# Summing the moved tiles of the last attention in SBUF rather than in DRAM

## The chip, the cores and the metric

The kernel runs on one core of a Trainium2 chip. The time is that of the device in microseconds, the median of three runs. TensorE (PE) multiplies matrices, VectorE (DVE) and ScalarE (ACT) work element by element, GpSimd (POOL) here hardly does more than issue transfers, and SyncE (SP) issues the plain loads and stores. Each engine takes its instructions in a fixed order.

## What is computed

Two graph layers on 4096 nodes with 512 features and a dense 4096 x 4096 adjacency mask. The first is an encoder and decoder with sigmoid attention in four heads. The second, in which the change lies, is a graph attention in four heads:

```python
feats  = einsum('nf,hfo->hno', X, W)
e_s    = einsum('hno,ho->hn', feats, a_self)
e_n    = einsum('hno,ho->hn', feats, a_neigh)
logits = e_s[:, :, None] + e_n[:, None, :]
logits = where(logits > 0, logits, 0.2 * logits)
logits = logits + NEG_INF * (1.0 - A)[None]
attn   = softmax(logits, axis=-1)
out    = einsum('hnm,hmo->hno', attn, feats)
out    = relu(out + b)          # then x = x + out
```

For each target node the weights over all source nodes are needed twice: multiplied with the features of the sources, and summed, since the softmax divides by their sum (the denominator).

## The kernel before

Three attentions (encoder, decoder, last) go through one function, `attention`. In the last, called at L788, a block is one head with one half of the targets: 4 heads x 2 halves of `TB` = 2048 targets make eight blocks, n = 0 to 7. A block runs over 32 tiles j of 128 sources. For each tile:

- SP loads a mask tile `a` (L198, 128 x 2048 bytes, five buffers).
- ScalarE makes the weights `e` (L761) from a row of the targets, `rowb`, and a column of the sources. In block 0 `rowb` is `row0`, a view of the tile `w` of 128 x 2048 floats; the later blocks load their own.
- VectorE multiplies by the mask (L762). Below, this is called the weighting of a tile.
- TensorE multiplies the features with the four slices of `e` into PSUM (L332, L329). The profile counts two instructions per product of float32.

The tiles `e` come from a rotation of nine buffers (`weight_tile`, L225).

The denominator is summed in three ways, divided by the constant `GAT` (L64). Tiles 14, 30 and 31 go through TensorE, multiplied by ones (L286). Eleven "moved" tiles (1, 3, 6, 8, 11, 13, 16, 18, 21, 23, 26) are summed by transfers that GpSimd issues (L344): the first is a plain store to `dacc[tb]`, a tile of 1 MiB in DRAM, the other ten add to it. There are two such tiles, one for each half of the targets, and so used by turns. At j = 30 the sum is read back into a weight tile `back` (L302). The other 18 are summed by VectorE into the tile `acc`, here a part of `R` (L350 for the first two, then L352). At the end of a block TensorE multiplies `back` and `acc` by ones as well (L286).

When a block is over, its sums leave PSUM on a chain of small transfers, all on GpSimd's queue, while the next block runs: ScalarE copies the sums (L235), `dens` is stored (L236) and loaded as a column `dcol` (L238), VectorE inverts it (L242, L243), `rinvs` is stored (L244), and four rows `rb` are loaded from it, spread over the partitions, two buffers by turns (L249). VectorE multiplies the block's output by them (L770), ScalarE adds the bias (L773), and GpSimd adds the result to the output in DRAM (L779). The last block ends without this chain.

Where these instructions stand in the order of each engine is decided by a scheduler when the program is built. A few places are tied by hand: `issue_after` keeps products and denominator products in a given order on TensorE.

The constants that matter are

```python
NJ = 32; TB = 2048; EP = 2; EVICT = 2      # e: EP + ebufs = 2 + 7 buffers
GAT = (1, 3, 6, 8, 11, 13, 16, 18, 21, 23, 26), (14, 30, 31)
```

Of the kernel before, what the change touches and what calls it, by code (L numbers as in the profile page):

```python
# [34 lines left out]
ALU = mybir.AluOpType  # L35
# [4 lines left out]
N, F, H, D, P = 4096, 512, 4, 128, 128  # L40
IB = 512
NIB = N // IB
NJ = N // P
C = IB // P

TB = 2048
# [10 lines left out]
TINY = 1e-30  # L57
# [6 lines left out]
GAT = (1, 3, 6, 8, 11, 13, 16, 18, 21, 23, 26), (14, 30, 31)  # L64
# [15 lines left out]
def kernel(ctx, tc, x, xT, adjT, w0, w0T, v0, wencT, wdecT, vecs, w1, w1T, a1, outT):  # L80
    nc = tc.nc
# [7 lines left out]
    R = [big.tile([P, N], FP, name=f"R{i}") for i in range(5)]  # L89
# [59 lines left out]
    dacc = [dram.tile([P, TB], FP, name=f"dacc{n}") for n in range(2)]  # L149
# [49 lines left out]


    def attention(what, keep, pools, weights, values, row_of, out, finish, ebufs, modes=None, invert=None,
                  kept=None, sums=None, extras={}, row0=None, masks0=()):

# [15 lines left out]
        spool, made, masks0 = pools, 0, list(masks0)  # L221
# [54 lines left out]
        for n, (h, tb) in enumerate(blocks):  # L276
            last = n == len(blocks) - 1
            moved, by_ones = modes(n) if modes is not None else ((), ())
            if invert is not None:
                den = bank1()  # L280
                begun = False

            def add_to_den(t, stop=False):
                nonlocal begun, last_ones
                for s in range(SB):
                    last_ones = nc.tensor.matmul(den[s * 32:(s + 1) * 32, :], ones[:, 0:32], t[:, s * IB:(s + 1) * IB],  # L286
                                                 start=not begun, stop=stop)
                begun = True

            po, ahead = [bank() for _ in range(SB - 1)], []  # L290
            adds, held, back, stores, next_row = [], [], None, [], None
            for j in range(NJ):
                for f in later.pop(j, []):
                    f()
                with tc.issue_after(a_load.ins) if j else nullcontext():
                    if (n, j) in extras:
                        extras[n, j]()
                    if not last and j == NJ - 10:
                        next_row = next_row_of(*blocks[n + 1])
                if moved and j == NJ - 2:  # L300
                    back = weight_tile()
                    nc.gpsimd.dma_start(back, dacc[tb])  # L302
                e = weight_tile()
                store = j % KEEP == KEEP - 1 and kept is not None
                if store and kept == "read":
                    a_load = nc.sync.dma_start(e, ekeep[h][tb][j // KEEP])
                else:
                    if masks0:
                        a, a_load = masks0.pop(0)
                    else:  # L310
                        a = mask_tile(keep)
                        a_load = load_mask(a, tb, j)
                    weights(e, rowb, a, j, h, SB if n + j == 0 else 1)
                    if store:
                        stores.append((j // KEEP, e))

                    if j % KEEP == KEEP - 3 and stores:
                        k, t = stores.pop()
                        nc.scalar.dma_start(ekeep[h][tb][k], t)

                def products():
                    nonlocal last_main, last_ones

                    with tc.issue_after(last_ones.ins) if last_ones is not None else nullcontext():

                        if j == EVICT:
                            po.append(bank())
                            for k, t in ahead:
                                nc.tensor.matmul(po[-1], block(values[h], k), t[:, (SB - 1) * IB:SB * IB],  # L329
                                                 start=(k == 0), stop=False)  # L330
                        for s, b in enumerate(po):
                            last_main = nc.tensor.matmul(b, block(values[h], j), e[:, s * IB:(s + 1) * IB],  # L332
                                                         start=(j == 0), stop=(j == NJ - 1))
                    last_ones = None


                early = last and j == NJ - 1 and invert is not None
                if not early:
                    products()
                if j < EVICT:  # L340
                    ahead.append((j, e))
                if invert is not None:
                    if j in moved:
                        nc.gpsimd.dma_start(dacc[tb], e, **({"accum_op": ALU.add} if j > moved[0] else {}))  # L344
                    elif j in by_ones:
                        held.append(e)
                    else:
                        adds.append(e)
                        if len(adds) == 2:
                            nc.vector.tensor_add(acc, *adds)  # L350
                        elif len(adds) > 2:
                            nc.vector.tensor_add(acc, acc, e)  # L352

                    if held and j + 1 not in by_ones:
                        with tc.issue_after(last_main.ins):
                            for t in held:
                                add_to_den(t)
                        held = []
                    if j == NJ - 1:
                        with tc.issue_after(last_ones.ins) if last_ones is not None else nullcontext():  # L360
                            if back is not None:
                                add_to_den(back)
                            add_to_den(acc, True)
                if early:
                    products()
            for k, t in stores:
                if last:
                    nc.scalar.dma_start(ekeep[h][tb][k], t)
                else:
                    at(EVICT, nc.scalar.dma_start, ekeep[h][tb][k], t)  # L370
            if not last:
                at(EVICT, lambda *block_end: ending(*block_end), h, tb, po, den if invert is not None else None)
                rowb = next_row
                continue
            outs = [out(spool, h, tb, s, po[s]) for s in range(SB)]
            if invert is None:
                for s, o in enumerate(outs):
                    rb = spread(h, tb, s)
                    for f in finish:
                        f(spool, h, tb, s, o, rb, True)  # L380
                continue

            inv = spool.tile([P, IB], FP, name="dsb")
            nc.vector.tensor_scalar(inv, den, invert[0], None, invert[1])
            nc.vector.reciprocal(inv, inv)
            if kept is not None:
                nc.gpsimd.dma_start(rinvs[h][tb].rearrange("o (s i) -> (o s) i", i=IB), inv[0:P:32, :])
            for s, o in enumerate(outs):
                rb = bank()
                nc.tensor.matmul(rb, ident[:, 32 * s:32 * s + 1].to_broadcast([P, P]), inv, start=True, stop=True)  # L390
                for f in finish:
                    f(spool, h, tb, s, o, rb, True)
# [13 lines left out]
    with tc.tile_pool(name="keep", bufs=1) as keep:  # L406

        with tc.tile_pool(name="f_small", bufs=1) as small, tc.tile_pool(name="f_work", bufs=2) as work:
# [5 lines left out]
            for ib in range(NIB):  # L414
# [7 lines left out]
                for c in range(0, C, 1 if ib == 0 else C):  # L422
                    n = 1 if ib == 0 else C
# [8 lines left out]
            for ib in range(NIB):  # L432
# [29 lines left out]
                for c in range(C):  # L462
                    j = ib * C + c
# [7 lines left out]
                if ib == SB - 1:  # L471
                    store_rows(rows[0], targets(0))
                    row0 = keep.tile([P, TB], FP, name="rowb", bufs=2)
                    row0_load = load_row(row0, rows[0], 0)
                    with tc.issue_after(row0_load.ins):
                        masks0 = []
# [39 lines left out]
        with tc.tile_pool(name="enc", bufs=1) as spool:  # L516

            with tc.issue_after(last_act.ins), tc.issue_after(masks0[-1][1].ins):
                attention("enc", keep, spool, tanh_weights, R[0:4], lambda h, tb: (rows[tb], h), out_enc,
                          (scaled, statistics), 7, lambda n: ENC if n > 1 else ENC_FIRST, (TINY, ALU.max), "write",  # L520
                          row0=row0, masks0=masks0,
                          extras={(2, 8): encoder_weights, (H * NTB - 1, NJ // 2): three_heads})
# [85 lines left out]
        with tc.tile_pool(name="dec", bufs=1) as spool:  # L608
            attention("dec", keep, spool, tanh_weights, xc, lambda h, tb: (rows[tb], h), out_dec, (scaled, elu), 4,
                      kept="read")  # L610
# [3 lines left out]
    with tc.tile_pool(name="l_small", bufs=1) as small, tc.tile_pool(name="l_work", bufs=2) as work:  # L614
# [82 lines left out]
        for ib in range(NIB):  # L697
            for c in range(C):
# [3 lines left out]
                j = ib * C + c  # L702
# [18 lines left out]
            if ib == SB - 1:  # L721
                store_rows(rows1[0], targets(0))
                row0 = w.rearrange("p c f -> p (c f)")
# [57 lines left out]
    with tc.tile_pool(name="gat", bufs=1) as spool:  # L781
        x1_last = []

        def load_last():
            x1_last.append(spool.tile([P, TB], FP, name="rowb", bufs=2))
            nc.sync.dma_start(x1_last[0], outT[(H - 1) * P:H * P, (NTB - 1) * TB:NTB * TB])

        attention("gat", spool, spool, gat_weights, v1, lambda h, tb: (rowsg, tb * H + h), out_gat,  # L788
                  (scaled_gat, add_to_output), 7, lambda n: GAT, (N * TINY, ALU.add), sums=R[2][:, 0:TB], row0=row0,
                  extras={(H * NTB - 1, NJ - 10): load_last})  # L790


# [40 lines left out]
```

## Time and profile before

| | us |
|---|---|
| median of three runs | 3400.32 |
| lowest, highest | 3393.2, 3400.7 |
| the profiled run, its span | 3400.29, 3398.4 |
| last attention, first weights to the end of the span | 2423.6 to 3398.4 |
| additions and stores to dacc (L344), whole kernel | 142, of 1 MiB each, 8.6 from issue to landing |
| read-backs (L302), whole kernel | 14, of 1 MiB each, 5.3 from issue to landing |

The decoder's attention sums nothing, as it uses what the encoder's kept. So the transfers of L344 and L302 are those of the encoder's and the last attention.

In a line of the timeline the columns are the start, the duration (both in us), the engine, the line of the kernel, the instruction, what it writes and reads and how often; in brackets stands how long the engine was idle before and what ended it. In a line of waits: who waited on which line, for what, how long in all, how often, and the longest. In a line by windows: the stretch, its length, the busy time with the number of instructions, the granted clock of TensorE, the share of the DMA engines and GB/s. The name of what ended a wait is inferred; where the engine named had long been done it was another.

### The profile page before, as it was taken

Reading aid. Unit: us, or ns where it says so; the run is one execution under the profiler, and the core shown is the slowest. Engines: PE = TensorE matmul, PEld = TensorE weight load, DVE = VectorE, ACT = ScalarE, POOL = GpSimd, SP = SyncE. Lnnn points to the kernel's source line nnn. Section 1 sums busy time; section 2 is a strip of 40 time slices with the busy share of each in tenths; the row PEclk is TensorE's granted clock in tenths of the full one; section 3 lists DMA queues with packets and bytes.
Section 4 is the critical chain, followed back from the end, with each engine's and each line's share of the span. In section 5 each row is a group of like instructions: output and inputs, shape, how many; then the busy total and the mean of one; then the engine's idle time right before and its main releaser. Section 6 shows DMA issues by size and latency. Waiting matters only on the chain.

```text
span 3398.4 us, 26074 instructions
## 1 busy us (share of the span) xinstructions
PE 3255.4 (96%) x8943; PEld 1501.3 (44%) x8943; DVE 2679.7 (79%) x1912; ACT 2598.4 (76%) x1908; POOL 325.5 (10%) x479
## 2 busy tenths in 40 slices
PE   7969999999999999999999999989999999999999
PEld 6423344344344464444444444448544344444443
DVE  6969799899898775665666556585699999999998
ACT  7969799999999438999999999565665564656553
POOL 2000000010010000000000000024201111111110
PEclk9989999999999999999999999989999999999999
DMA  9994578778777103434444344231388788788876
GB/s 190 195 158 146 163 225 241 205 214 240 208 227 200 55 13 136 142 130 138 145 141 136 133 139 139 62 127 69 94 206 205 186 216 192 196 207 201 208 187 169
DMA packets 180309, 559.60 MB, mean 165 GB/s; under 512 B 20372, under 2 KB 23700, under 8 KB 144208
## 3 DMA queue, kind: packets, MB, share of 16 engines
q0 software_dynamic: 43232, 211.14, 31.7%
q1 hardware_dynamic: 126288, 293.66, 25.8%
q10 hardware_dynamic: 10656, 53.15, 3.9%
q8 instruction: 70, 1.15, 0.1%
q14 instruction: 63, 0.52, 0.0%
HBM read 391.78 MB, written 233.19 MB: 184 GB/s over the span
## 4 chain that ended last, share of the span: by engine, by line
PE 57%; DVE 19%; DMA 11%; issue 9%; ACT 3%; POOL 1%; DVEq 0%; ACTq 0%; POOLq 0%
PE ps L332 42%; DVE e L762 7%; PE ps L533 6%; DMA a<-mask 5%; DVE R L352 5%; DVE e L402 4%; PE ps L707 3%; DMA rb<-rinvs 3%; DMA rinvs<-dcol 1%; PE den L286 1%; DVE acc L352 1%; ACT e L401 1%; ACT e L400 1%; PE ps L467 1%; PE ps L588 1%
## 5 line engine op out<-in xcount | busy, mean ns | idle before, releaser
L332 PE MATMUL ps<-e,R 128*128 128x512 f32 x6048 | 2661.4, 601 | 104.3 <-DVE e L402 70.9
L332 PEld LDWEIGHTS ps<-e,R 128*128 128x128 f32 x6048 | 1155.8, 192 | 1600.2 <-issue 1437.4
L402 DVE TENSOR_TENSOR e<-e,a 128x2048 f32<-128x2048 f32 (+1 forms) x470 | 1050.2, 2259 | 372.5 <-ACT e L401 348.3
L400 ACT ACTIVATE e<-rowb,score 128x2048 f32<-128x2048 f32 (+1 forms) x470 | 913.5, 1968 | 82.4 <-PE ps L332 46.6
L401 ACT ACTIVATE e<-e 128x2048 f32<-128x2048 f32 (+1 forms) x470 | 872.8, 1882 | 44.1 <-DVE e L402 37.6
L761 ACT ACTIVATE e<-rowb,nq,jcol 128x2048 f32<-128x2048 f32 x224 | 454.6, 2085 | 206.9 <-DMA dacc<-e 165.0
L762 DVE SCALAR_TENSOR_TENSOR e<-e,jcol,a 128x2048 f32<-128x2048 f32 (+1 forms) x259 | 589.7, 2316 | 3.8 <-DMA a<-mask 2.6
L352 DVE TENSOR_TENSOR R<-R,e 128x2048 f32<-128x2048 f32 x128 | 291.5, 2278 | 0.0
L352 DVE TENSOR_TENSOR acc<-acc,e 128x2048 f32<-128x2048 f32 x126 | 288.1, 2287 | 2.2
L344 POOL DMA_DIRECT2D dacc<-e x142 | 117.8, 830 | 1087.9 <-DMA dacc<-e 432.7
L533 PE MATMUL ps<-R,w 128*128 128x512 f32 x512 | 220.3, 592 | 0.6 <-DVE w L501 0.6
L249 POOL DMA_DIRECT2D rb<-rinvs x88 | 47.9, 547 | 1135.4 <-DVE R L491 874.5
L533 PEld LDWEIGHTS ps<-R,w 128*128 128x128 f32 x512 | 97.2, 190 | 122.7 <-issue 117.9
L773 ACT ACTIVATE R<-R,vec 128x512 f32<-128x512 f32 x32 | 23.1, 722 | 142.2 <-DVE R L770 141.7
L707 PE MATMUL ps<-w1x,hT 128*128 128x260 f32 x512 | 117.5, 388 | 2.8 <-ACT hT L683 2.8
L553 ACT ACTIVATE ex<-ps,bias 128x512 f32<-128x512 f32 x64 | 44.1, 688 | 97.5 <-PE ps L533 80.4
L707 PEld LDWEIGHTS ps<-w1x,hT 128*128 128x128 f32 x512 | 97.7, 193 | 22.8 <-ACT hT L683 4.4
L286 PE MATMUL den<-e,ones 128*32 128x512 f32 x784 | 93.6, 598 | 0.0
L761 ACT ACTIVATE e<-w,nq,jcol 128x2048 f32<-128x2048 f32 (+1 forms) x35 | 65.6, 1938 | 35.7 <-DMA dacc<-e 32.4
L491 DVE TENSOR_TENSOR R<-R,rb 128x512 f32<-128x512 f32 x60 | 40.5, 686 | 51.6 <-DMA rb<-rinvs 39.4
L555 DVE SCALAR_TENSOR_TENSOR ex<-ex,re 128x512 f32<-128x512 f32 x64 | 45.0, 703 | 36.2 <-ACT re L554 36.1
L712 ACT ACTIVATE R<-ps,rstd 128x128 f32<-128x128 f32 x128 | 38.6, 368 | 39.8 <-PE ps L707 38.9
(154 smaller groups left out, 1209.1 us busy)
## 6 DMA issues: line engine op xcount, KB each, us to landing
a<-mask SPq DMA_DIRECT2D x720, 256.0 KB, 3.3
dacc<-e POOLq DMA_DIRECT2D x142, 1024.0 KB, 8.6
ekeep<-e ACTq DMA_DIRECT2D x48, 1024.0 KB, 9.4
e<-ekeep SPq DMA_DIRECT2D x48, 1024.0 KB, 4.9
rb<-rinvs POOLq DMA_DIRECT2D x88, 256.0 KB, 3.8
mask<-in_adjT POOLq DMA_DIRECT2D x8, 2048.0 KB, 117.6
rowb<-rows SPq DMA_DIRECT2D x16, 1024.0 KB, 6.7
e<-dacc POOLq DMA_DIRECT2D x14, 1024.0 KB, 5.3
```

The source lines that it names most:

```text
L249: nc.gpsimd.dma_start(rb, everywhere(rinvs[h][tb], 0, s * IB, IB))
L286: last_ones = nc.tensor.matmul(den[s * 32:(s + 1) * 32, :], ones[:, 0:32], t[:, s * IB:(s + 1) * IB], start=not begun, stop=stop)
L332: last_main = nc.tensor.matmul(b, block(values[h], j), e[:, s * IB:(s + 1) * IB], start=(j == 0), stop=(j == NJ - 1))
L344: nc.gpsimd.dma_start(dacc[tb], e, **({"accum_op": ALU.add} if j > moved[0] else {}))
L352: nc.vector.tensor_add(acc, acc, e)
L400: nc.scalar.activation(e, rowb, AF.Tanh, bias=column(score[:, 1], j, h), scale=0.5)
L401: nc.scalar.activation(e, e, AF.Exp, scale=0.5)
L402: nc.vector.tensor_mul(e, e, a)
L533: nc.tensor.matmul(z, w[:, fb, o * P:(o + 1) * P], nodes(src[fb], ib), start=(fb == 0), stop=(fb == C - 1))
L707: nc.tensor.matmul(b[:, 0:2 * DX], hT[:, fb, c * P:(c + 1) * P], w1x[:, fb, 2 * k:2 * k + 2, :].rearrange("p h x -> p (h x)"), start=(fb = ...
L761: nc.scalar.activation(e, rowb, AF.Relu, bias=column(nq, j, h), scale=column(jcol, j, h))
L762: nc.vector.scalar_tensor_tensor(e, e, column(jcol2, j, h), a, ALU.add, ALU.mult)
```

## The change

`attention` gets one more tile, `sums2`. Where it is given, the moved tiles of every block but the first are summed into it instead of `dacc[tb]`; it lies in SBUF, so it isn't read back, and TensorE multiplies it by ones where it took `back`. The last attention gives `row0` for it, which holds the targets' row of block 0 and is free after that. Block 0 still goes through DRAM, as do the encoder's blocks. The seven blocks 1 to 7 share one `sums2`.

```diff
-                if moved and j == NJ - 2:
+                moved_sum = dacc[tb] if n == 0 or sums2 is None else sums2
+                if moved and moved_sum is not sums2 and j == NJ - 2:
                     back = weight_tile()
                     nc.gpsimd.dma_start(back, dacc[tb])
...
                     if j in moved:
-                        nc.gpsimd.dma_start(dacc[tb], e, **({"accum_op": ALU.add} if j > moved[0] else {}))
+                        nc.gpsimd.dma_start(moved_sum, e, **({"accum_op": ALU.add} if j > moved[0] else {}))
...
-                            if back is not None:
+                            if moved and moved_sum is sums2:
+                                add_to_den(sums2)
+                            elif back is not None:
                                 add_to_den(back)
                             add_to_den(acc, True)
...
         attention("gat", spool, spool, gat_weights, v1, lambda h, tb: (rowsg, tb * H + h), out_gat,
-                  (scaled_gat, add_to_output), 7, lambda n: GAT, (N * TINY, ALU.add), sums=R[2][:, 0:TB], row0=row0,
+                  (scaled_gat, add_to_output), 7, lambda n: GAT, (N * TINY, ALU.add), sums=R[2][:, 0:TB],
+                  sums2=row0, row0=row0,
```

More of the change, by code (lines that the diff above doesn't have):

```diff
@@ L201, in attention @@
     def attention(what, keep, pools, weights, values, row_of, out, finish, ebufs, modes=None, invert=None,
-                  kept=None, sums=None, extras={}, row0=None, masks0=()):
+                  kept=None, sums=None, sums2=None, extras={}, row0=None, masks0=()):
         spool, made, masks0 = pools, 0, list(masks0)
```

## The prediction

> **What bounds the kernel now.** I began with the page: over the whole span TensorE and VectorE are both nearly full, so shares settle nothing.
>
> ```profile
> PE 3255.4 (96%) x8943; PEld 1501.3 (44%) x8943; DVE 2679.7 (79%) x1912; ACT 2598.4 (76%) x1908; POOL 325.5 (10%) x479
> ```
>
> The change acts in the last attention alone, so I cut that into its eight blocks. I call T0 the moment when TensorE ends the denominator products (L286, on the tile R) of a block; in the timeline of TensorE these fall at 2545.2, 2662.5, 2784.0, 2907.2, 3029.2, 3146.6, 3265.8 and 3384.3 us. Between them lie the blocks n = 1 to 7. The view by windows, for VectorE, with busy time and granted clock:
>
> ```profile
> 2545.20:2662.50 117.30, 112.58 (x56) 1.00 0.85 206
> 2662.50:2784.00 121.50, 113.55 (x56) 0.99 0.83 202
> 2784.00:2907.20 123.20, 112.60 (x56) 0.97 0.81 196
> 2907.20:3029.20 122.00, 113.54 (x57) 0.97 0.83 202
> 3029.20:3146.60 117.40, 110.71 (x55) 1.00 0.85 200
> 3146.60:3265.80 119.20, 113.38 (x56) 0.99 0.85 205
> 3265.80:3384.30 118.50, 104.58 (x52) 0.97 0.78 184
> ```
>
> The sum is 839.1 us, 119.9 a block, of which VectorE works 112 to 113 (the last window lacks records). Next, who waits for whom over these seven blocks:
>
> ```profile
> DVE dcol L242 <- DMA dcol<-dens: 28.3, 5, 7.1
> DVE R L770 <- DMA rb<-rinvs: 24.4, 7, 6.7
> PE ps L332 <- DVE e L762: 26.0, 10, 6.4
> ```
>
> VectorE stands still for two things only: the column dcol and the row rb, by which the block before is normalized, 52.7 us or 7.5 a block. It never waits for ScalarE or a weight buffer. So its period is 112.3 + 7.5. TensorE then starves for what VectorE made late. Its own work shows where it does not starve:
>
> ```profile
> 2790.95 31.06 PE L332 MATMUL ps<-e,R 128*128 128x512 f32 x72
> 2828.41 15.68 PE L332 MATMUL ps<-e,R 128*128 128x512 f32 x32 [6.41 <-DVE e L762]
> 2845.02 58.63 PE L332 MATMUL ps<-e,R 128*128 128x512 f32 x136
> ```
>
> 58.63 us for 136 is 0.431 each; a weight tile takes 8 (3.45 us). With 256 in a block (110.4) and 40 of the denominator (24 in 2.78, 8 in 1.04, 8 in 1.06: 4.9) TensorE needs 115.2 us. The shortest block confirms it: 117.3 less gaps of 1.40, 0.56 and 0.27 is 115.1. Up to 4.7 us a block can thus be won before TensorE binds.
>
> Why do dcol and rb come late? The timeline of GpSimd (POOL), block n = 5, T0 = 3029.2:
>
> ```profile
> 3024.94 0.55 POOL L344 DMA_DIRECT2D dacc<-e  x1 [9.97 <-DVE e L762]
> 3030.56 0.86 POOL L344 DMA_DIRECT2D dacc<-e  x1 [5.07 <-DMA dacc<-e]
> 3031.53 0.57 POOL L236 DMA_DIRECT2D dens<-dsb  x1
> 3039.33 0.57 POOL L238 DMA_DIRECT2D dcol<-dens  x1 [7.23 <-DMA dens<-dsb]
> 3040.72 0.88 POOL L344 DMA_DIRECT2D dacc<-e  x1 [0.81 <-DVE e L762]
> 3045.42 0.56 POOL L244 DMA_DIRECT2D rinvs<-dcol  x1 [3.82 <-DVE dcol L243]
> 3049.40 0.86 POOL L344 DMA_DIRECT2D dacc<-e  x1 [3.42 <-DMA dacc<-e]
> 3050.14 1.23 POOL L249 DMA_DIRECT2D rb<-rinvs  x2
> ```
>
> The small transfers of the chain dens, dcol, rinvs, rb stand in one queue with the megabyte additions. Each addition waits at the head for the one before; a small one issued just behind it lands with it: dens 7.8 us after issue, rb 8.3 (VectorE takes it at 3058.42, after 6.69 us of standing).
>
> **What the Trainium skill says.** "DMA: Bandwidth & Descriptors", section "Rules for kernel authors": accumulating transfers go from GpSimd, and another access to the same bytes must wait for the earlier one's semaphore, in HBM or in SBUF. So the serial chain stays; the trace agrees, with 8 to 10 us between additions. The same page, "Queues, rings and completion order": each DMA engine consumes descriptors in ring order. The trace agrees: dcol lands in 1.9 us when the ring is empty, in 8.3 us (block 3) 0.6 us behind an addition. The same page, "Anatomy of one DMA": 2.0 us plus bytes at 436 GB/s, the receipt slowest from HBM. For 1 MiB that is 4.4 us (read-back here: median 5.1 in the stage); for the two megabytes that an addition reads I estimate 6.8 from it (measured into DRAM: 8.2). "SBUF — State Buffer", "SBUF: two separate sides": engine accesses and DMA don't slow each other; no addition into SBUF is in this trace to check it.
>
> **The change part by part.** Line numbers are those of before.
>
> Removed: seven read-backs (L302) with their tile, a megabyte each, 5.0 to 5.9 us from issue to landing. They land some 5 us before the denominator products take them (block 3: issued 2893.14, taken from 2903.58) and nothing is queued behind them but the next block's additions, so their time is hidden: worth 0. The weight tile saved is worth 0 directly, as VectorE never waits for one, but the scheduler puts one more weighting ahead of L350 in blocks 4 to 7 (nine in a row for eight).
>
> Kept in number: 77 additions and stores at L344, now into SBUF. The trace has no such addition. From below: 5.6 us, what the plain store of dacc takes; the estimate 6.8 lies between. From above: 12, the longest addition at L344. I take 9 near the chain's small transfers (10.2 between additions in blocks 3 and 5, 8.5 to 9.0 in 6 and 7), that is no change: reads from HBM go, but more passes through SBUF's ports.
>
> Added: one wait. Two buffers by turns become one, so the first store of a block (tile 1) can't start before TensorE has read the sum, at about T0 - 1. Before, it went at T0 - 4.3 in block 5, - 2.5 in 1 and 2, - 3.3 in 3 and 4. Behind it on GpSimd stand dens, whose input is ready only at T0 too, and the other additions. The added product waits for the addition of tile 26 instead of a read-back; those were issued 19.6 to 23.4 us before the next T0 and landed 11 to 15 before it, so it costs 0. SP's queue is the same in both built programs.
>
> Moved: in the built program the order on GpSimd in blocks 4 to 7 is tile 1, dens, tile 3, dcol, tile 6, rinvs, tile 8, rb, rb; before, two or three additions stood ahead of dens. VectorE's order shifts as well: more weightings before L242 and L770.
>
> The sum for blocks 4 to 7, from T0: store of tile 1 at 0.3, landed at 5.9, with dens just behind (issued at 3.7, as in block 3). Tile 3 goes at 6.0, dcol at about 7.5, landing with it at 15. VectorE comes to dcol at 6.7 (L350 in block 5) + 2.3 (the extra weighting) + four instructions of 2.25 = 18, so it stands for nothing. Tile 6 goes at 15, rinvs at 20.5 and lands by 24.5; tile 8 goes at 24, rb at 25.2 and lands behind it, 8.3 later: 33.5. VectorE, five instructions further, reaches L770 at 29.6 and stands 3.9 us. Does TensorE notice? In the new order tile 12 is the first weighted after two L770 and one addition, 5.7 us after rb: 39.2. TensorE wants it at 12 x 3.45 = 41.4. No gap. The same sum on before, block 3: rb at T0 + 36.4, then 7.9 us up to tile 11: 44.3, against 38.0 wanted, a gap of 6.3; the trace has 6.41.
>
> Block 3 keeps eight in a row: tile 11 is made at 39.2 against 38.0 and loses 1.2: 116.4. Block 2 has rb ahead of tile 8, lands it near 27 and loses next to nothing: 115.5. Block 1 has the old order on both engines and only the later start: rb at about 29 against 26.8, so 119.5. Seven blocks: 119.5 + 115.5 + 116.4 + 4 x 115.2 = 812.2, or 26.9 less than 839.1. Gaps of 0.3 to 0.6 us a block at the ends, as seen in blocks 1, 2 and 5, take back 4: **23 us**. The span was 3398.4 and its run 3400.29, in line with the median 3400.32 (3393.2 to 3400.7): 3400 - 23 = **3377 us**.
>
> **The rivals.**
> *The chain only moves (no change).* If rb lands at T0 + 40 rather than 33.5, since transfers of out or the masks hold the ring, VectorE stands as long as before and the period stays 119.9: 3400 us. For it: the start is 3 to 5 us later and four transfers still stand ahead of rb. Against it: dens no longer waits behind two additions, and more work covers the wait.
> *The additions into SBUF are longer (slower).* One mechanism: ten additions and a store in series must now fit between one T0 and the next. It decides from about 11 us each: 0.3 + 6 + 110 + 2 = 118.3, and rb by then at T0 + 39.5. At 12 the block is 128.3 and the whole 3400 + 7 x 8.4 = 3459 us. For it: two reads and a write meet in SBUF. Against it: the estimate of 6.8 and HBM's part gone.
> *Additions as short as 6.8.* rb lands 6 us sooner, no block starves, 7 x 115.2: 3367 us. This is the forecast's better end.
> That the change doesn't do what it says is next to excluded: the built program shows the seven sums in w.
>
> **How the numbers follow.** The forecast with its better end has 0.67 (3364 to 3390), no change 0.20, slower 0.13. No change spills 0.04 into faster and 0.01 into slower. About 0.3% (10 us) is what a measurement here can tell from no change: faster 0.71, same 0.15, slower 0.14. The range goes from all gaps closed and short additions, 3364, to no change with its spread, 3403; outside lie the slow rival and a little below.
>
> **What would show it.** Right: no wait at L242, under 4 us a block at L770, blocks of 115 to 116 us, L332's waits for L762 under 8 us in all. The step on additions is wrong if they take over 10.5 us; the step on the chain if rb comes after T0 + 37; the claim that read-backs are hidden if TensorE's ends of blocks change without any change in VectorE's waits.

## The result, and the profile after

The changed kernel takes 3361.48 us (median of four runs, 3357.54 to 3367.73); before, with one run more than was shown above, 3396.76 us (3389.08 to 3400.7). The ratio is 0.9901, 95% interval 0.9875 to 0.9926: 35 us or 1.0% faster. The prediction had the sign and the mechanism, 3377 us with a range of 3364 to 3403; the time lies 2.5 us below that range. The interval, applied to 3396.8, runs from 3354 to 3372 us, so the edge of the range is within the noise; but it stands for a gain of 25 to 42 us, and the forecast was 23.

The profiled run has a span of 3358.9 us against 3398.4. The line numbers are now higher (L332 became L334, L762 L766, L770 L774, L344 L346). The totals on the page hardly move:

```profile
PE 3239.6 (96%) x8943; PEld 1496.2 (45%) x8943; DVE 2680.2 (80%) x1912; ACT 2599.2 (77%) x1908; POOL 323.4 (10%) x472
```

The ends of the denominator products, T0, now fall at 2541.05, 2657.33, 2772.47, 2888.92, 3003.75, 3118.58, 3233.40 and 3344.80. The view by windows for VectorE, columns as before:

```profile
2541.05:2657.33 116.28, 112.60 (x56) 1.00 0.82 196
2657.33:2772.47 115.14, 112.54 (x56) 1.00 0.83 201
2772.47:2888.92 116.45, 112.54 (x56) 1.00 0.83 199
2888.92:3003.75 114.83, 112.92 (x56) 1.00 0.83 201
3003.75:3118.58 114.83, 112.67 (x56) 1.00 0.83 202
3118.58:3233.40 114.82, 113.17 (x56) 1.00 0.83 203
3233.40:3344.80 111.40, 104.32 (x52) 1.00 0.80 190
```

The sum is 803.75 us against 839.1: 35.4 us, all of the change. The other 4.1 us between the two spans lie before 2545 us, where both programs are the same; all but two of the kernels below reached this first T0 from 2539.8 to 2545.2 us (the two at 2534.4 and 2550.9), so 4 us there are no more than that scatter. VectorE's busy time in a block is what it was. Its waits are not:

```profile
DVE R L774 <- DMA rb<-rinvs: 18.3, 10, 3.9
DVE dcol L243 <- DMA dcol<-dens: 0.4, 1, 0.4
PE ps L334 <- DVE e L766: 2.0, 4, 0.6
```

52.7 us of standing became 18.7, and TensorE's gaps fell from 26.0 to 2.0. In block 5 TensorE has none, from one T0 to the next; from its timeline:

```profile
3010.65 44.80 PE L334 MATMUL ps<-e,R 128*128 128x512 f32 x104
3055.38 1.06 PE L287 MATMUL den<-e,ones 128*32 128x512 f32 x8
3056.37 58.63 PE L334 MATMUL ps<-e,R 128*128 128x512 f32 x136
```

GpSimd in the same block, T0 = 3003.75:

```profile
3003.22 0.56 POOL L346 DMA_DIRECT2D w<-e  x1 [23.73 <-PE den L287]
3006.09 0.57 POOL L237 DMA_DIRECT2D dens<-dsb  x1 [2.31 <-ACT dsb L236]
3008.69 0.91 POOL L346 DMA_DIRECT2D w<-e  x1 [2.03 <-DMA w<-e]
3009.27 0.89 POOL L239 DMA_DIRECT2D dcol<-dens  x1
3017.58 0.87 POOL L346 DMA_DIRECT2D w<-e  x1 [7.42 <-DMA w<-e]
3025.89 0.57 POOL L245 DMA_DIRECT2D rinvs<-dcol  x1 [7.44 <-DVE dcol L244]
3026.45 0.90 POOL L346 DMA_DIRECT2D w<-e  x1
3027.89 1.12 POOL L250 DMA_DIRECT2D rb<-rinvs  x2 [0.54 <-DMA rinvs<-dcol]
```

The store of tile 1 goes at T0 - 0.5, when TensorE has read the sum. Most of the 23.7 us that GpSimd stands idle ahead of it is time in which tile 1 isn't made yet: in block 1, where there is no sum to wait for, it goes at T0 - 2.5, and in before it went at T0 - 2.5 to - 4.3. So the wait itself is 2 to 4 us long; its effect is that dens now goes ahead of the additions of tiles 3 and 6. dens is issued at T0 + 2.3 to 2.9 in blocks 4 to 7 (before: 11.9 to 14.3 in blocks 4, 6 and 7), and dcol lands at T0 + 13.1 to 14.5. VectorE asks for it at T0 + 19.3 in block 5. In before it asked at T0 + 16.6 to 17.5 in blocks 4, 6 and 7 and got it at 21.7 to 23.8, after up to 7.1 us of standing. So dcol now lands ahead even of the times at which before asked.

The row rb moves less. VectorE's first L774 is at T0 + 31.7, 32.9, 31.3 and 31.1 in blocks 4 to 7, 31.8 on average, where L770 was at 34.3, 29.2, 32.5 and 34.4, 32.6 on average: sooner in three blocks and 3.7 us later in block 5, which nevertheless lost its gap. What differs there is what VectorE has made by then. VectorE, block 4 of before (T0 = 2907.2; block 5 did not stand for dcol):

```profile
2914.80 2.28 DVE L350 TENSOR_TENSOR R<-e 128x2048 f32<-128x2048 f32 x1
...
2930.91 0.17 DVE L242 TENSOR_SCALAR dcol<-dcol 128x16 f32<-128x16 f32 x1 [7.11 <-DMA dcol<-dens]
...
2941.48 0.69 DVE L770 TENSOR_TENSOR R<-R,rb 128x512 f32<-128x512 f32 x1 [1.35 <-DMA rb<-rinvs]
```

and block 5 of after (T0 = 3003.75):

```profile
3014.14 2.29 DVE L352 TENSOR_TENSOR R<-e 128x2048 f32<-128x2048 f32 x1
...
3023.07 0.17 DVE L243 TENSOR_SCALAR dcol<-dcol 128x16 f32<-128x16 f32 x1
...
3036.65 0.69 DVE L774 TENSOR_TENSOR R<-R,rb 128x512 f32<-128x512 f32 x1 [2.16 <-DMA rb<-rinvs]
...
3040.06 4.61 DVE L766 SCALAR_TENSOR_TENSOR e<-e,jcol,a 128x2048 f32<-128x2048 f32 x2
```

In before tile 11 was the first to be weighted after rb, here tile 12 is: made at 3042.3, T0 + 38.6, and wanted by TensorE at T0 + 41.4. TensorE no longer notices the chain.

### The profile page after: what moved, and what is told of

Its sections match the earlier page's. It is cut to its first block, busy times and chain, and to the rows that moved or that the text cites. A ratio compares the mean times of both kernels' runs of the same rounds, so it can differ in the third digit from the quotient of the medians.

```text
span 3358.9 us, 26058 instructions
## 1 busy us (share of the span) xinstructions
PE 3239.6 (96%) x8943; PEld 1496.2 (45%) x8943; DVE 2680.2 (80%) x1912; ACT 2599.2 (77%) x1908; POOL 323.4 (10%) x472
## 4 chain that ended last, share of the span: by engine, by line
PE 69%; DVE 13%; DMA 9%; issue 7%; ACT 2%; POOL 0%; DVEq 0%; SPq 0%; POOLq 0%; ACTq 0%
PE ps L334 54%; PE ps L537 7%; DVE e L406 4%; DVE e L766 4%; PE ps L711 3%; DVE R L354 3%; DMA rb<-rinvs 3%; DMA a<-mask 3%; PE den L287 2%; DMA rinvs<-dcol 1%; DVE acc L354 1%; PE ps L592 1%; ACT e L405 1%; DMA w<-e 1%; DMA mask<-in_adjT 1%
## 5 line engine op out<-in xcount | busy, mean ns | idle before, releaser
L334 PE MATMUL ps<-e,R 128*128 128x512 f32 x6048 | 2645.9, 598 | 81.1 <-DVE e L406 71.4
L334 PEld LDWEIGHTS ps<-e,R 128*128 128x128 f32 x6048 | 1151.1, 191 | 1567.3 <-issue 1433.3
L766 DVE SCALAR_TENSOR_TENSOR e<-e,jcol,a 128x2048 f32<-128x2048 f32 (+1 forms) x259 | 590.3, 2320 | 3.8 <-ACT e L765 3.8
L346 POOL DMA_DIRECT2D w<-e x77 | 65.2, 847 | 549.9 <-DVE e L766 178.2
L346 POOL DMA_DIRECT2D dacc<-e x65 | 53.8, 827 | 571.4 <-DVE e L406 259.8
```

What stands on the lines that cost most here:

```text
L346: nc.gpsimd.dma_start(moved_sum, e, **({"accum_op": ALU.add} if j > moved[0] else {}))
L766: nc.vector.scalar_tensor_tensor(e, e, column(jcol2, j, h), a, ALU.add, ALU.mult)
```

## The experiments

Four theories. **A**: the added wait changes the order in which GpSimd and VectorE have their instructions, so that VectorE's two waits are covered. **B**, later **D** for what A leaves over: the place of the sums (shorter additions, or no read-back). **C**: the weight buffer that the read-back no longer takes. "Stage" is the sum of the seven blocks in the profile (before 839.1, after 803.8). "Median" is followed by that of before from the same set of runs. The line numbers in each kernel shift with its edits.

### The wait alone, in DRAM

```diff
-  nc.gpsimd.dma_start(dacc[tb], e, ...)
+  put = nc.gpsimd.dma_start(dacc[tb], e, ...)
+  if what == "gat" and n and j == moved[0]:
+      tc.add_manual_dep(put.ins, den_end.ins.name, ...)   # the block before: last product of add_to_den(acc, True)
```

> Before, with one thing added: in blocks 1 to 7 the store of tile 1 waits until TensorE has ended the sums of the block before. Sums stay in two tiles in DRAM, read back as before. Theory A (the place in the queue): the gain came because that wait lets dens and dcol go ahead of the additions of tiles 3 and 6. In this built program they do: tile 1, dens, tile 3, dcol. Then rb lands near T0 + 33.5, the first tile weighted after two L770 is tile 12, and TensorE has no gap: 3360 to 3368 us. Theory B (the place of the sums: additions into SBUF are shorter, and no read-back takes the ring): no gain, 3390 to 3410 us, as only a wait was added. Theory C (the weight buffer that the read-back gives up): no gain, 3397 us.

Measured: 3378.0 us (before 3397.1), ratio 0.9947 (0.9932 to 0.9961), stage 819.0. A wait that shortens nothing gains 19 us with the sums still in DRAM; B and C, which expected none, are out as the main cause. Of VectorE's two waits, the one for dcol is all but gone, and the one for rb has grown from 24.4 us:

```profile
DVE R L775 <- DMA rb<-rinvs: 34.2, 7, 5.9
DVE dcol L242 <- DMA dcol<-dens: 1.6, 1, 1.6
```

The gain is short of A's numbers too. GpSimd in block 5, T0 = 3012.83:

```profile
3028.26 0.87 POOL L344 DMA_DIRECT2D dacc<-e  x1 [8.03 <-DVE R L356]
3036.65 0.86 POOL L344 DMA_DIRECT2D dacc<-e  x1 [7.52 <-DMA dacc<-e]
3037.19 0.88 POOL L244 DMA_DIRECT2D rinvs<-dcol  x1
3045.85 1.10 POOL L249 DMA_DIRECT2D rb<-rinvs  x2 [7.78 <-DMA rinvs<-dcol]
```

The addition of tile 8 stands ahead of rinvs here, and rb reaches VectorE only at T0 + 36.8. The scheduler's order is a part of the effect and has to be held in later runs.

### SBUF without the wait: two tiles by turns

```diff
-  sums2=row0, row0=row0,
+  sums2=(row0, spool.tile([P, TB], FP, name="sums3")), row0=row0,
...
-  moved_sum = dacc[tb] if n == 0 or sums2 is None else sums2
+  moved_sum = dacc[tb] if n == 0 or sums2 is None else sums2[n % 2]
```

> After, with two tiles in SBUF by turns, so that tile 1 need not wait for the sums of the block before. No read-back, one weight buffer more to spare. In the built program two or three additions again stand ahead of dens, as in before. Theory A: dcol and rb come late again, VectorE stands 6 to 9 us a block: 3385 to 3400 us. Theory B: the whole gain, 3355 to 3365 us. Theory C: the whole gain too, as nine weightings stand ahead of the first addition in four blocks: 3355 to 3365 us.

Measured: 3392.7 us (3397.1), ratio 0.9987 (0.9979 to 0.9996), stage 835.5. Everything that the change was about is in this kernel: additions into SBUF, no read-back, the spare buffer. It gains 4 us. VectorE stands 49.8 us in all, against 52.7 before:

```profile
DVE dcol L243 <- DMA dcol<-dens: 31.4, 7, 7.0
DVE R L775 <- DMA rb<-rinvs: 18.4, 7, 3.8
```

This is A's number, and against B and C.

### The copy kept: SBUF, one tile, read back

```diff
-  if moved and moved_sum is not sums2 and j == NJ - 2:
+  if moved and j == NJ - 2:
       back = weight_tile()
-      nc.gpsimd.dma_start(back, dacc[tb])
+      nc.gpsimd.dma_start(back, moved_sum)
...
-  if moved and moved_sum is sums2:
-      add_to_den(sums2)
-  elif back is not None:
+  if back is not None:
```

> After, but the sum in SBUF is copied to a weight tile by a transfer, as the read-back did, and TensorE takes the copy. The tile of sums is then free before T0, and in the built program two or three additions stand ahead of dens, in the order of before. Theory A: no gain, 3390 to 3400 us. Theory B, if the shorter addition is what counts: a gain of 15 to 35 us, 3362 to 3382 us; if only the missing read-back counts: no gain. Theory C: no gain.

Measured: 3388.2 us (3397.1), ratio 0.9973 (0.9962 to 0.9984), stage 832.5. A little better than A's 3390 to 3400 and far from B's 3362 to 3382. With the copy the tile is free before T0, the order of before comes back, and VectorE stands 27.5 us for dcol and 19.4 for rb. This kernel reads back and is 4.5 us under the one with two tiles, which does not; their orders differ, so this prices nothing, but it shows no cost of the read-backs.

### The chain moved to SP

```diff
+  small = nc.sync if what == "gat" else nc.gpsimd
-  nc.gpsimd.dma_start(dens[h][tb], dsb[0:P:32, :])
+  small.dma_start(dens[h][tb], dsb[0:P:32, :])
...    # likewise dcol, rinvs and rb
```

> Before, with the small transfers of the last attention (dens, dcol, rinvs, rb) issued by SP and not by GpSimd; additions and read-backs as before, in DRAM. Theory A: the chain no longer stands behind additions, VectorE stands for under 2 us a block, TensorE binds at 115 us a block: 3358 to 3366 us. If the chain's delay is in the DMA engines and not in the queue, it keeps a half of its wait: 3375 to 3385 us. Theories B and C: 3397 us, or slower by masks that wait behind the chain on SP.

Measured: 3373.8 us (3397.1), ratio 0.9937 (0.9922 to 0.9952), stage 821.2, with the other edits of the change absent. So what stands ahead in GpSimd's queue is a cause. The first two blocks take 114.8 us each and the third 115.5: TensorE binds, as expected. From block 4 on they take 117 to 122, for two reasons. First, dens now stands on SP behind mask loads that wait for VectorE. Block 5:

```profile
2996.41 13.90 SPq L198 DMA_DIRECT2D a<-mask  x7
3010.35 0.51 SPq L237 DMA_DIRECT2D dens<-dsb  x1
3014.24 0.32 SPq L239 DMA_DIRECT2D dcol<-dens  x1
```

T0 was 3001.45: dens, ready about 3 us after it, is issued after 8.9. Second, another queue doesn't take a small transfer out from behind an addition. In block 4 an addition goes on GpSimd's queue and dcol 0.6 us later on SP's, and VectorE stands for it:

```profile
2892.89 0.86 POOL L345 DMA_DIRECT2D dacc<-e  x1 [7.59 <-DVE e L763]
2893.49 0.32 SPq L239 DMA_DIRECT2D dcol<-dens  x1
2900.93 0.17 DVE L243 TENSOR_SCALAR dcol<-dcol 128x16 f32<-128x16 f32 x1 [6.18 <-DMA dcol<-dens]
```

dcol took 7.4 us to land here, and 6.9 and 7.1 in blocks 6 and 7, where it was issued 1.1 and 0.8 us behind an addition. In blocks 2, 3 and 5 no addition had just been issued, and it took 1.6 to 1.8 (for block 1 the profile has no landing). VectorE still stands 18.8 us for dcol and 17.6 for rb, where A allowed for under 2 us a block, so A's first case failed. The result lies between the two cases, 1 us from the one in which the delay is in part in the DMA engines.

### The wait, with GpSimd's order held

```diff
+  with tc.issue_after(rinvs_put.ins) if what == "gat" and n and j == 8 else nullcontext():
       put = nc.gpsimd.dma_start(dacc[tb], e, ...)      # in the kernel with the wait alone
```

> The run with the wait alone gained 18 us, half of the change's 34, but its built order differs from that of after: the addition of tile 8 stands ahead of rinvs, and rb comes at T0 + 36.8 (after: T0 + 32.9). Here the same kernel (DRAM, two tiles, read-back, the wait) with one tie more: the addition of tile 8 is issued after rinvs. Built order on GpSimd: tile 1, dens, tile 3, dcol, tile 6, rinvs, tile 8, rb. Theory A (place in the queue): rb near T0 + 33, eight weightings ahead of the first addition, so tile 11 is the first after two L770, made at 38.7 against 38.0: a gap of about 1 us a block, 3364 to 3371 us. Theory D (the rest of the gain is the place of the sums or the missing read-back): as with the wait alone, 3375 to 3381 us.

Measured: 3376.0 us (3397.7), ratio 0.9931 (0.9916 to 0.9946), stage 817.1. rb now comes at T0 + 33.2 to 33.8 in blocks 4 to 7, as expected, and TensorE's gaps there are 1.0 to 1.7 us; yet it lies 5 us above A's range and inside D's. VectorE stands 1.9 us for dcol, but 31.3 for rb. Something was left over.

### The buffer, alone and with the wait

Both change one number in the call of the last attention: to the kernel of before, and to the kernel with the held order.

```diff
-  (scaled_gat, add_to_output), 7, lambda n: GAT, ...
+  (scaled_gat, add_to_output), 8, lambda n: GAT, ...
```

> Before with a tenth weight buffer in the last attention and nothing else. In the built program nine weightings stand ahead of the first addition, but three or four additions ahead of dens. Theory A: the buffer alone moves nothing, since the chain is what VectorE waits for: 3388 to 3398 us. Theory C (the buffer): a gain of 15 us or more, under 3382 us.

> The run wait_order with a tenth weight buffer in place of the one that the read-back takes, so that nine weightings stand ahead of the first addition in blocks 4 to 7, as in after. Order on GpSimd is that of after; sums in DRAM, read back. Theory A with the buffer: no gap, the whole gain, 3358 to 3366 us. Theory D: not under 3372 us, as the sums are still in DRAM.

Measured: on before, 3403.8 us (3397.7), ratio 1.0019 (1.0010 to 1.0027), stage 847.8, 6 us slower where A allowed for nothing or a small gain. VectorE stands more for dcol:

```profile
DVE dcol L242 <- DMA dcol<-dens: 39.8, 7, 12.7
```

since three additions now stand ahead of dens in blocks 4 to 6, and four in block 7. With the wait and the held order, 3375.1 us (3397.7), ratio 0.9929 (0.9915 to 0.9944), stage 817.9: no different from the same kernel without the buffer, against A's 3358 to 3366 and as D had it (not under 3372). VectorE's order in this kernel still was not that of after: L242 and L243 stood one instruction later each, and so rinvs went at T0 + 24.7 in block 5 and not at 22.1. So the buffer by itself is out as the cause; the next kernel keeps it, and what the order there gives without a tenth buffer wasn't run.

### VectorE's order held too

```diff
+  tied = what == "gat" and n > 2 and j in (5, 7)
+  with tc.issue_after(cols[j // 7].ins) if tied else nullcontext():     # cols: L242 and L243
       nc.vector.tensor_add(acc, acc, e)
...
+  with tc.issue_after(cols[1].ins) if what == "gat" and n > 3 and j in (10, 11) else nullcontext():
       weights(e, rowb, a, j, h, ...)
```

> The run wait_order_slot (3375 us; sums in DRAM, read back) with VectorE's order tied to that of after in blocks 4 to 7: dcol one addition and one weighting earlier, two weightings later. VectorE's order is then that of after throughout, GpSimd's too but for the read-back and the wait in block 1. What is left of a difference to after (3361) is the place of the sums and the read-back. Theory A, with VectorE's order counted in: 3358 to 3366 us. Theory D: 3369 to 3377 us, rb still 2 us or more later than in after.

(The shift named there is too large: in the built orders it is one instruction for L242 and for L243.) Measured: 3367.1 us (3396.0), ratio 0.9915 (0.9901 to 0.9929), stage 810.4. Sums in DRAM and read back, but VectorE's order that of after and GpSimd's too, save for the read-backs; one wait more, in block 1: 29 us of the change's 34 to 35. VectorE stands 24.2 us for rb, where it stood 32.0 in the kernel before this (L779 is the L774 of after):

```profile
DVE R L779 <- DMA rb<-rinvs: 24.2, 11, 4.8
DVE dcol L243 <- DMA dcol<-dens: 1.8, 1, 1.8
```

It lies 1 us outside A's range and below D's. Blocks 4 to 6 take 115.9, 116.5 and 115.7 (after: 114.8).

### The place of the sums alone

```diff
-  put = nc.gpsimd.dma_start(dacc[tb], e, ...)       # in the kernel with GpSimd's order held
+  put = nc.gpsimd.dma_start(moved_sum, e, ...)      # sums2 = row0 in blocks 1 to 7, copied to back at j = 30
```

> The run wait_order (3376 us) with the sums of blocks 1 to 7 in SBUF (one tile, copied to a weight tile at the end as the read-back was); the order of every instruction on every engine is the same as in wait_order. Only the place of the sums differs. If the place counts (theory D: shorter additions, by 0.4 us and more each, so that rb comes 1 to 2 us sooner): a gain of 7 to 14 us on wait_order, 3362 to 3369 us. If only the place in the queue counts: 3373 to 3379 us.

Measured: 3370.5 us (3396.0), ratio 0.9924 (0.9910 to 0.9937), stage 811.4, between the two expectations. As the pair's intervals overlap, both went on one chip once more:

> The kernel wait_order again (sums in DRAM), beside the next one on one chip, since the two were 3376.0 and 3370.5 us but measured at different times, with intervals that overlap. Theory D in its small form (the place of the sums is worth 4 to 6 us, 0.15%): this one 4 to 6 us above the next. Theory A alone: the two within 2 us of each other.

> The kernel sbuf_wait_order again (sums in SBUF, copied at the end; the order on every engine that of wait_order), on the chip of the run before. Theory D in its small form: 4 to 6 us below it. Theory A alone: within 2 us of it.

Measured: in DRAM 3373.0 us (3370.2 to 3374.5), in SBUF 3369.2 (3366.4 to 3371.0), before 3397.1; ratios 0.9926 (0.9914 to 0.9939) and 0.9918 (0.9904 to 0.9931); stages 815.2 and 810.7. In both pairs SBUF is lower, by 5.5 and 3.8 us in the median and by 5.7 and 4.5 in the stage; the last five runs of each overlap a little. So D's small form is nearly met (3.8 for 4 to 6), and A's 2 us are exceeded. The additions and stores, in the view of transfers (count, KB, median us to landing), DRAM and then SBUF:

```profile
dacc<-e POOLq DMA_DIRECT2D x75, 1024.0 KB, 8.5
```

```profile
w<-e POOLq DMA_DIRECT2D x76, 1024.0 KB, 7.9
```

So the place is worth some 4 to 6 us here. The shorter additions are the likely way: rb comes 0.8 to 1.0 us sooner on average in blocks 4 to 7. The kernel with both orders held leaves 6.7 us of the stage over; 1.3 of it is the wait in block 1, and the rest is about what the place was worth, if it is worth the same there, which wasn't run. What the read-back is worth was not separated; little is left for it.

### A twelfth moved tile

TensorE binds in blocks 4 to 6 of after, so I tried to relieve it.

```diff
-  GAT = (1, 3, 6, 8, 11, 13, 16, 18, 21, 23, 26), (14, 30, 31)
+  GAT = (1, 3, 6, 8, 10, 13, 15, 17, 19, 22, 24, 26), (30, 31)
```

> After, with tile 14 taken from TensorE's sums and a twelfth tile moved by transfer instead (moved: 1, 3, 6, 8, 10, 13, 15, 17, 19, 22, 24, 26; by ones: 30, 31). If TensorE now binds at 114.8 us in blocks 4 to 6: eight products of 0.13 us less a block, 1.0 us, times eight: 3361 - 8 = 3353 us. If the transfers' chain binds instead (twelve of 8.3 to 9 us, 100 to 108 us, plus the wait at T0): no gain or a loss, 3361 to 3375 us. If VectorE binds (112.3 plus 2 to 4 of waits): 3358 to 3363 us.

Measured: 3374.9 us (3397.7), ratio 0.9929 (0.9914 to 0.9944): 13 us behind after, and no expected case puts it so high but the second. The stage takes 811.4, with VectorE standing 24.7 us for rb, 4.6 for dcol and 4.7 for TensorE's sums. The stage is only a part of the loss: the first T0 comes at 2550.9, 9.8 us later than in after, so more is lost ahead of it, where block 0 has the new lists too. Which of the reordered instructions is to blame wasn't taken apart. The change as it stands remains the fastest kernel of the study.

## Why the prediction was right or wrong

**Which unit binds, and by how much**: right. VectorE's work without waits was put at 112.3 and TensorE's at 115.2; the profile after has 112.5 to 113.2 and 114.83. One reading was wrong: the last window of before doesn't lack records. After has the same 52 instructions there, and in both 29 weightings for 33 in the other windows: four tiles of the next block are weighted before a T0, and behind block 7 there is no next block.

**What is removed costs nothing**: not contradicted for the read-backs, which no run took away with the orders held. For the buffer: alone it gains nothing, as said.

**Kept in number**: additions near the chain were taken at 9 us, and those of tiles 3 and 6 do stand 8.7 to 9.2 us apart in blocks 4 to 7. Over all additions the medians are 7.9 to 8.0 in SBUF, 8.4 to 8.5 in DRAM for the same order: "no change" was off by half a microsecond, and the estimate of 6.8 was too low. That a column lands with the addition ahead of it was read as the order within one ring. The kernel with the chain on SP has nearly the same delay across two queues, so that order alone is not the reason. The forecast does not hang on it, as the chain stays on GpSimd.

**The added wait and the moved instructions**: right in blocks 4 to 6. Predicted: rb at T0 + 33.5, tile 12 at 39.2, no gap. Block 5 had 32.9, 38.6 and none. That rb fits so well is in part luck: rinvs goes at T0 + 22.1 and not at 20.5, but lands in 1.7 us and not in 4, and the two errors nearly cancel. The runs show two parts of the reason. The order on GpSimd takes away the wait for dcol: 28.3 us of standing become 1.6 to 2.1 in all kernels with the wait in DRAM. The order on VectorE puts one more tile ahead of rb, and with it the gain goes from 21 to 24 us to 29, beside which rb comes only 0.8 us sooner on average in after. Of the signs of being right that the prediction named, all came but the length of the last block: 0.4 us in all at L242, 2.6 a block at L770, 2.0 in all at L332, blocks of 114.8 to 116.5.

**The sum**: here it failed. The terms for block 7, for block 1 and for the gaps at the ends were too long. Against 812.2 us plus the 4 taken back, 816.2, the stage took 803.8, 12.4 less:

- *"4 x 115.2" for blocks 4 to 7*: 3.8 us in block 7. In the last block the denominator products stand ahead of the products of the last tile (`early` in the code), so its T0 comes one tile, 3.45 us, sooner. Before had this too, so 115.2 set a full block against a short one. Block 7 should have had 115.2 - 3.45, about 111.7; it took 111.4.
- *Block 1, "119.5"*: 3.2 us. It took 116.3. I gave it the later start, but block 1 is the first to use the tile: no sum of a block before is to be read from it, so it waits for nothing. With a real wait there it takes 117.3 to 118.7 (five kernels with the sums in DRAM), so even that would have cost 0 to 1.3 us over before's 117.3, and not 2.2.
- *"Gaps ... take back 4"*: 4 us. The gaps came to 2.0 in all, and they lie in blocks 1 and 3, whose figures held such gaps already.
- Blocks 2 and 4 to 6 were 0.4 us each too long: 1.5 in all. Block 3 was right, 116.4 and 116.45.

The remaining 3.5 us of the miss are the median of before, which went from 3400.3 to 3396.8 with one run more (3396.0 to 3397.7 in the later sets of 9 to 18 runs). All the larger errors were to the same side, and so the lower end of the range, 3364, was too near: short additions were the only thing that it allowed for, and the sum itself had no slack downwards.

**The rivals**: the chain that only moves didn't come: rb, which it put at T0 + 40, came at 31.1 to 32.9. Longer additions didn't come. The better end of 3367 was closest, but for the wrong reason: additions took 7.9 to 8.0 us and not 6.8, and rb came no 6 us sooner.

## What to carry to other kernels

When each engine's order is fixed at build time, ask of every wait what stands ahead of it on its own engine and on the queue that serves it; a change of buffers can move both, and here the kernel with the edit's purpose but not its side effect gained 4 us of 35. A separate queue keeps a small transfer from standing behind additions that are not yet issued, but here not from landing with the one in flight. Compare the built orders first, and experiment on one with the other held. When a sum is made over blocks, do the first and the last by themselves: their waits and their order are not those of the middle ones.

## What I had not expected of the hardware

An addition of 1 MiB into SBUF takes 7.9 us against 8.4 to 8.5 into DRAM with the same order on GpSimd and VectorE: leaving DRAM saves only 6 to 7%. A column of 8 KB issued close behind such an addition on the same queue takes 7.5 to 8.4 us to land (medians of six kernels, in SBUF as in DRAM), against 1.9 with nothing ahead of it. Issued on SP's queue 0.6 to 1.1 us behind an addition on GpSimd's, it takes 6.9 to 7.4 us, and 1.6 to 1.8 where no addition had just been issued.
